# Heads of 16 and layer 0's experts: six call sites of a tiled matrix product, four pieces of 32 columns in place of two of 64

## The chip, the cores and the metric

The kernel runs on one core of one Trainium2 chip. Its time is the device time of one execution in microseconds (us). Five engines work side by side and meet at semaphores: TensorE (PE in the profile, its weight loads listed apart as PEld), VectorE (DVE), ScalarE (ACT), GpSimd (POOL) and SyncE (SP), which here mainly issues DMAs. Lower is better. All matrices are float32; the profile records each float32 matmul of the program as two weight loads and two matmuls.

## The reference, cut to what matters

A decoder of two layers on `x` of 8 batches x 256 tokens x 256 features. Each layer has self-attention with 16 heads of 16 features, a cross-attention to `ctx_2048`, and a mixture of experts. The part that the change touches:

```python
x = x + L0_attn(layernorm(x))     # q, k, v = x @ W.T + b; rope; softmax; @ Wo.T + bo
x = x + L0_xattn(ctx, layernorm(x))   # 16 heads of 16, no projections
x = x + L0_ffn(layernorm(x))      # below
x = x + L1_attn(layernorm(x))     # as L0_attn, causal, no biases
x = x + L1_xattn(layernorm(x), ctx)   # 16 heads of 64: not touched
x = x + L1_ffn(layernorm(x))      # 8 routed experts and a shared one: not touched

def L0_ffn(x):
    gates = einsum("bnd,de->bne", x, gate_w)
    t = log(clip(gates, 1e-6))
    for _ in range(8):            # Sinkhorn: columns, then rows
        t = t - logsumexp(t, axis=-2); t = t - logsumexp(t, axis=-1)
    vals, idx = top_k(swapaxes(exp(t), -1, -2), N // E)   # 32 tokens for each expert
    out = einsum("ebmd,edf->ebmf", x[idx], experts) * vals
    return zeros.at[idx].set(out)
```

## The kernel before

**Stages.** `plain` holds the whole work in order. Its first stage, up to about 467 us of the trace, runs 24 units: for each pair of batches of layer 0 two self-attentions and two cross-attentions, and then layer 1's eight self-attentions. Beside them go the experts of layer 0. After it come layer 1's cross-attention with heads of 64 and the last experts, which the change does not touch.

**One unit.** A unit (`SelfAttention` or `CrossAttention`, with a `Core`) has four steps, 0 to 3. In a step, `Core.scores` (L328, tile `st`) makes four matmuls of 32 rows x 128 columns of the array, 512 moving columns each; ScalarE takes the exponential of them (L339, tile `pT`); `Core.values` (L365, tile `o`) makes eight matmuls of 128 rows x 32 columns. One step's records are thus 8 of `st` and 16 of `o`. The scores of the next step are issued ahead of the values of this one, so that ScalarE's exponentials run beside TensorE's other work.

**What goes between.** All other TensorE work of the stage is put into these steps by hand: `beside(n, k, at, ...)` names a unit, a step and a place, `run(n, k, early)` issues what is planned (early: between scores and values; else after values). So the usual order on TensorE is scores, values, then whatever the plan put there, then the next scores. The order of all five engines in the stage is the order of the code (`tc.manual_schedule(engines=PINNED)`, L913). What is put there:

- `heads` (tile `qk`, 512 wide) and `vals` (tile `v`, 256 wide) through `projected`: x normalised and transposed, times Wq, Wk and Wv; `out` (tile `ao`, 256 wide): the attention's output times Wo, added to `x`.
- `transposed`, `begin`, `CrossAttention.out`: transposes on the full 128 x 128 array (tiles `tr`, `qps`, `qpsx`, `oR`).
- `chosen_experts`, a generator of which each `yield` ends a piece, one generator for two batches, so four in all: gates (tile `lg`, 8 wide), eight Sinkhorn iterations (tile `cs`, 16 wide, each a matmul with ones and then five operations on VectorE), the choice of tokens (VectorE and two DMAs), gathering the rows by a matmul with a one-hot matrix (tile `rps`), the experts themselves (tile `y`, L721, matmuls of 128 rows x 32 columns), and the return of the rows (tile `back`).

**The helper.** All products above but those of `st`, `o`, `y` and the transposes go through `product` (L274 to L278), whose matmuls all carry line L276. It cuts the 128 columns of the stationary operand `lhsT` in two halves of 64; each half is a matmul of its own, on its own half of the array's columns and of the output's partitions. `start` and `stop` open and close the accumulation. `product` is used in the later stages too (tiles `k`, `v<-wkv_x`, `h`, `wo`, `sc` and others), by call sites that stay as they are.

Of the kernel before, what the change touches and what calls it, by code (L numbers as in the profile page):

```python
# [39 lines left out]
P = 128  # L40
# [3 lines left out]
HP = 32  # L44
CTX = 512
XH, XD = 16, 64
E = 8
# [110 lines left out]
def plain(  # L158
# [4 lines left out]
    nc = tc.nc  # L163
# [53 lines left out]
    ones = const.tile([P, P], F32, name="ones")  # L217
# [46 lines left out]
    def layernorm_T(b, work, mm, bufs=2):  # L264

        xn = work.tile([P, 2, D], F32, tag="xn", name="xn", bufs=bufs)
        mv, rs = norm_stats([x[:, 2 * b + t, :] for t in range(2)], 1e-5, small, "ln")
        for t in range(2):
            last = normed(xn[:, t, :], x[:, 2 * b + t, :], mv, rs, t)
        return last, transposed(xn, work, mm, "xnT", bufs=bufs)  # L270
# [3 lines left out]
    def product(out, lhsT, rhs, start, stop):  # L274
        return [
            nc.tensor.matmul(out[h], lhsT[:, h], rhs, start=start, stop=stop, skip_group_check=True)  # L276
            for h in (slice(0, 64), slice(64, P))
        ]  # L278

    def transposed(rows, work, mm, tag, dst=None, bufs=2):  # L280

        ps = mm.tile([P, 2, 2 * P], F32, tag="mm", name="tr")
        for t in range(2):
            for c in range(2):
                nc.tensor.transpose(ps[:, c, t * P : (t + 1) * P], rows[:, t, c * P : (c + 1) * P], ident)  # L285
        if dst is None:
            dst = work.tile([P, 2, 2 * P], F32, tag=tag, name=tag, bufs=bufs)
        nc.scalar.copy(dst, ps)  # L288
        return dst
# [130 lines left out]
    class SelfAttention:  # L420
# [17 lines left out]
        def rows(self):  # L438
            self.xnT = transposed(self.xn, work, mm, "xnT")
            self.qkr = work.tile([P, 2, 2 * D], F32, tag="qkr", name="qkr")  # L440

        def projected(self, ps, t, lo, hi):
            for c in range(2):
                product(ps, self.xnT[:, c, bass.ts(t, P)], self.w[:, c, lo:hi], c == 0, c == 1)

        def heads(self, t):
            qk = mm.tile([P, 2 * D], F32, tag="mm", name="qk")
# [16 lines left out]
        def begin(self):  # L464
            kT = transposed(self.qkr[:, :, D:], work, mm, "kT")
            qps = mm.tile([P, 2, S], F32, tag="mm", name="qps")
            for t in range(2):
                for c in range(2):
                    nc.tensor.transpose(qps[:, c, bass.ts(t, P)], self.qkr[:, t, bass.ts(c, P)], ident)
            qm = masked_queries(work, qps, mask2)  # L470
            mine = dens[:, 2 * self.layer, 2 * self.b : 2 * self.b + 2]
            self.core = Core(kT, qm, self.v_pad, 1.0 / math.sqrt(HD), self.layer == 1, None, mine)
# [7 lines left out]
        def out(self, t):  # L480
            b, attT = self.b, self.core.attT
            xt = x[:, 2 * b + t, :]
            ps = mm.tile([P, 2 * D], F32, tag="mm", name="ao")[:, :D]
            for c in range(2):
                product(ps, attT[:, c, bass.ts(t, P)], self.wo[:, c, :], c == 0, c == 1)
            nc.vector.tensor_tensor(xt, xt, ps, ALU.add)


# [102 lines left out]
    gate = one.tile([P, 2, E], F32, name="gate")  # L591
# [35 lines left out]
    def chosen_experts(b0, nb):  # L627

        xn = bwork.tile([P, 2 * nb, D], F32, tag="xnb", name="xnb")
        g = bwork.tile([P, nb, 2, E], F32, tag="g", name="g")  # L630
# [10 lines left out]
        for b, xnT in enumerate(xnTs):  # L641
            lg = mm.tile([P, 2, D], F32, tag="mm", name="lg")
            for t in range(2):
                for c in range(2):
                    product(lg[:, t, :E], xnT[:, c, bass.ts(t, P)], gate[:, c, :], c == 0, c == 1)
            nc.vector.tensor_scalar(g[:, b], lg[:, :, :E], 1e-6, None, ALU.max)
            yield

        gt = bwork.tile([P, 2, nb, E], F32, tag="gt", name="gt")
        for it in range(8):  # L650
            cs = mm.tile([P, nb, E], F32, tag="mm", name="cs")
            for t in range(2):
                product(cs, ones, g[:, :, t, :], t == 0, t == 1)
            rc = bwork.tile([P, nb, E], F32, tag="rc", name="rc")
            nc.vector.reciprocal(rc, cs)
            nc.vector.tensor_tensor(g, g, rc.unsqueeze(2).to_broadcast([P, nb, 2, E]), ALU.mult)
            rsum = bwork.tile([P, nb, 2], F32, tag="rsum", name="rsum")
            nc.vector.tensor_reduce(rsum, g, AX.X, ALU.add)
            rr = bwork.tile([P, nb, 2], F32, tag="rr", name="rr")
            nc.vector.reciprocal(rr, rsum)  # L660
            dst = gt.rearrange("p t b e -> p b t e") if it == 7 else g
            nc.vector.tensor_tensor(dst, g, rr.unsqueeze(3).to_broadcast([P, nb, 2, E]), ALU.mult)
            yield
# [36 lines left out]
        def picked(b):  # L700
            pick = bwork.tile([P, 2, S], F32, tag="pick", name="pick")
            for t in range(2):
                nc.gpsimd.tensor_scalar(pick[:, t, :], idx_row[:, b, :], tokid[:, t : t + 1], None, ALU.is_equal)
            picks.append(pick)
# [3 lines left out]
        for b in range(nb):  # L708
            pick, put = picks[b], bwork.tile([P, 2, S], F32, tag="put", name="put")
            rps = mm.tile([P, 2, S], F32, tag="mm", name="rps")  # L710
            for c in range(2):
                for t in range(2):
                    product(rps[:, c, :], xn[:, 2 * b + t, bass.ts(c, P)], pick[:, t, :], t == 0, t == 1)
            rT = bwork.tile([P, 2, S], F32, tag="rT", name="rT")
            rows_made = nc.scalar.copy(rT, rps)
            yield
            y = mm.tile([P, 2, D], F32, tag="mm", name="y")
            for e in range(E):
                rows = slice(TOP * (e % 4), TOP * (e % 4) + TOP)
                for c in range(2):  # L720
                    nc.tensor.matmul(  # L721
                        y[rows, e // 4, :],
                        rT[:, c, TOP * e : TOP * (e + 1)],
                        experts[:, e, c, :],
                        start=c == 0,
                        stop=c == 1,
                    )
            for h in range(2):
                q = 2 * b + h
                junk = bwork.tile([P, S], F32, tag="junk", name="junk")  # L730
                for made in (
                    nc.gpsimd.tensor_scalar(put[:, h, :], num, col[:, 0, q : q + 1], None, ALU.is_equal),
                    nc.vector.scalar_tensor_tensor(
                        junk,
                        idx_row[:, b, :],
                        col[:, 0, q : q + 1],
                        later[:, h, :],
                        ALU.is_equal,
                        ALU.mult,
                        accum_out=over[:, q : q + 1],  # L740
                    ),
                ):
                    tc.add_manual_dep(made.ins, rows_made.ins.name, apart, reason="one entry's at a time")
            of_b = slice(2 * b, 2 * b + 2)
            nc.vector.tensor_scalar(weight[:, of_b], over[:, of_b], 0.0, None, ALU.is_equal)
            nc.vector.tensor_tensor(weight[:, of_b], weight[:, of_b], col[:, 1, of_b], ALU.mult)
            ys = bwork.tile([P, 2, D], F32, tag="ys", name="ys")
            for h in range(2):
                q = 2 * b + h
                nc.vector.tensor_scalar(ys[:, h, :], y[:, h, :], weight[:, q : q + 1], None, ALU.mult)  # L750
            if b + 1 < nb:
                picked(b + 1)
            yield
            back = mm.tile([P, 2, D], F32, tag="mm", name="back")
            for t in range(2):
                for h in range(2):
                    product(back[:, t, :], put[:, h, bass.ts(t, P)], ys[:, h, :], h == 0, h == 1)
            xb = x[:, 2 * (b0 + b) : 2 * (b0 + b) + 2, :]
            nc.vector.tensor_tensor(xb, xb, back, ALU.add)
            yield  # L760
# [93 lines left out]
    for n, u in enumerate(units):  # L854
# [28 lines left out]
    start = begun + (  # L883
        (0, 2, EARLY), (0, 3, 40), (0, 3, 41), (1, 0, 70), (1, 2, 70),
        (1, 3, 70), (2, 0, 15), (2, 1, 5), (2, 2, 10), (2, 2, 70), (2, 3, 70), (3, 0, 70), (3, 1, 45),
        (3, 2, 70), (3, 3, 85),
    )
# [1954 lines left out]
```

## Time and profile before

| | |
|---|---|
| median of 3 runs | 1226.51 us (1221.11 to 1227.33) |
| the profiled execution's own time | 1223.53 us |
| its span, first to last instruction | 1221.8 us |
| instructions | 28741 |
| PE busy in the span | 1152.2 us, 94% |
| PE busy from 10 to 470 us | 418.30 of 460 us, 4266 matmul records |
| of it the records of line L276 | 170.25 us, 1400 records |
| DVE / ACT / POOL busy from 10 to 470 us | 294.51 / 242.25 / 213.18 us |

In rows of instruction groups, a form such as `128*64 128x256` is a matmul on 128 rows and 64 columns of the array with 256 moving columns; matmuls on different columns of the array run side by side. "x256 | 33.4, 387" is 256 records, in whose union the engine was busy 33.4 us, 387 ns each. Since records overlap, the time that a record costs is the busy time over the count (or the distance of two starts), not its own duration. In the timeline, consecutive records of one kind are merged into one row with its start, its length and its count.

### The profile page before, as it was taken

The page shows a single profiled execution, that of the slowest core. Times are in us where ns is not written, and L with a number is a line of the kernel's source. Part 1 is how long each engine was busy: PE and PEld are TensorE (multiplying, and loading weights), DVE is VectorE, ACT ScalarE, POOL GpSimd, SP SyncE. Part 2 cuts the span into 40 slices and gives each one's busy share as a digit, 9 for nine tenths or more (in the row PEclk, how much of TensorE's full clock was granted, in tenths as well). Part 3 has the DMA queues.
Part 4 walks back from the last instruction along what each step waited for, and adds up shares of the span by engine and source line. Part 5 has one row for each costly group of instructions (what it writes and reads, how often), then busy time and mean ns, then how long its engine had stood idle before and what let it go on. Part 6 is the DMA issues. An engine that isn't in the chain of part 4 may idle for free.

```text
span 1221.8 us, 28741 instructions
## 1 busy us (share of the span) xinstructions
PE 1152.2 (94%) x12188; PEld 710.1 (58%) x12188; DVE 563.1 (46%) x1564; ACT 447.9 (37%) x696; POOL 416.9 (34%) x482
## 2 busy tenths in 40 slices
PE   5899989999898998999999999999999999999996
PEld 2334444444454444576666666666666576888874
DVE  4455767757776656223332423333335474222113
ACT  2666655656334351223232323232323231222220
POOL 2334344442736642032423333241416115000013
PEclk8999999999999999999999999999999999999999
DMA  7036232040200330010101010101012108599934
GB/s 221 1 119 211 89 104 93 10 169 1 82 1 11 104 132 2 18 37 18 36 19 37 18 36 19 36 19 36 19 37 72 35 6 322 233 393 410 378 104 128
DMA packets 51434, 116.58 MB, mean 95 GB/s; under 512 B 8272, under 2 KB 36416, under 8 KB 46944
## 3 DMA queue, kind: packets, MB, share of 16 engines
q1 hardware_dynamic: 45120, 98.90, 23.7%
q0 software_dynamic: 3456, 12.73, 2.9%
q10 hardware_dynamic: 2720, 3.02, 0.7%
q8 instruction: 98, 1.61, 0.5%
q14 instruction: 40, 0.33, 0.1%
HBM read 104.00 MB, written 27.93 MB: 108 GB/s over the span
## 4 chain that ended last, share of the span: by engine, by line
PE 75%; POOL 7%; DVE 7%; issue 5%; ACT 3%; DMA 1%; SPq 0%; POOLq 0%; DVEq 0%; ACTq 0%
PE v L276 7%; PE h L276 7%; PE k L276 6%; PE wo L276 5%; PE ox L1452 5%; PE stx L1413 4%; PE st L328 4%; PE out L1830 4%; PE qk L276 3%; PE o L365 3%; PE h L1035 3%; PE out L1647 3%; PE q L276 3%; PE tr L285 2%; PE fm L276 2%
## 5 line engine op out<-in xcount | busy, mean ns | idle before, releaser
L339 ACT ACTIVATE pT<-st 128x1024 f32<-128x1024 f32 (+1 forms) x128 | 110.5, 917 | 83.0 <-PE st L328 82.2
L365 PE MATMUL o<-pT,padv 128*32 128x256 f32 (+1 forms) x1536 | 100.0, 372 | 3.2 <-POOL pT L344 3.1
L1419 POOL TENSOR_TENSOR both<-pTx 128x512 f32<-128x512 f32 x64 | 82.1, 1309 | 48.9 <-issue 43.2
L365 PEld LDWEIGHTS o<-pT,padv 128*32 128x32 f32 x1536 | 40.8, 110 | 86.3 <-issue 41.7
L276 PE MATMUL h<-xrT,w 128*64 128x128 f32 (+1 forms) x1936 | 87.2, 250 | 2.9 <-issue 2.9
L258 POOL TENSOR_TENSOR lnrs<-lnve,mhalf 128x2 f32<-128x2 f32 x48 | 34.7, 724 | 157.2 <-DVE lnve L256 152.8
L276 PEld LDWEIGHTS h<-xrT,w 128*64 128x64 f32 x1936 | 84.5, 137 | 5.9 <-issue 3.7
L339 ACT ACTIVATE pT<-st,kbias 128x1024 f32<-128x1024 f32 x64 | 67.8, 1112 | 40.2 <-PE st L328 40.2
L1417 ACT ACTIVATE pTx<-stx 128x1024 f32<-128x1024 f32 x64 | 62.1, 1021 | 41.3 <-PE stx L1413 26.2
L1028 DVE TENSOR_TENSOR midr<-sl,h 128x128 f32<-128x128 f32 x102 | 29.4, 288 | 102.2 <-PE h L276 68.6
L328 PE MATMUL st<-qm,kT 32*128 32x512 f32 (+1 forms) x512 | 69.1, 610 | 5.1 <-ACT pT L339 3.2
L1027 ACT ACTIVATE sl<-h 128x128 f32<-128x128 f32 (+1 forms) x114 | 35.3, 310 | 99.3 <-PE h L276 58.5
L276 PE MATMUL qk<-l_wqkv,xnT 128*64 128x512 f32 x256 | 65.4, 634 | 2.2 <-ACT xnT L288 2.2
L1413 PE MATMUL stx<-qTx,kTx 64*128 64x256 f32 x512 | 64.3, 391 | 2.5 <-ACT pTx L1417 2.5
L1452 PE MATMUL ox<-pTx,vx 128*64 128x256 f32 x512 | 62.3, 385 | 0.0
L1507 POOL TENSOR_TENSOR oT<-oT,rs 128x512 f32<-128x512 f32 x30 | 37.7, 1290 | 67.0 <-DMA rs<-rd 67.0
L258 POOL TENSOR_TENSOR lxrs<-lxve,mhalf 128x2 f32<-128x2 f32 x8 | 5.6, 703 | 153.5 <-DVE sc L1166 123.3
L276 PE MATMUL wo<-wout_x,oT 128*64 128x256 f32 x512 | 58.0, 379 | 0.0
L1413 PEld LDWEIGHTS stx<-qTx,kTx 64*128 64x128 f32 x512 | 46.1, 186 | 20.3 <-ACT pTx L1417 7.2
L344 POOL TENSOR_SCALAR_AFFINE_SELECT pT<-pT 128x512 f32<-128x512 f32 x64 | 41.5, 661 | 41.8 <-ACT pT L339 41.8
L1452 PEld LDWEIGHTS ox<-pTx,vx 128*64 128x64 f32 x512 | 33.9, 136 | 26.4 <-issue 12.1
L1460 DVE COPY oT<-ox 128x512 f32<-128x512 f32 x16 | 11.1, 691 | 81.0 <-PE ox L1452 81.0
(361 smaller groups left out, 2198.3 us busy)
## 6 DMA issues: line engine op xcount, KB each, us to landing
w<-packs SPq DMA_DIRECT2D x22, 1408.0 KB
w<-packs SPq DMA_DIRECT2D x22, 768.0 KB
rs<-rd SPq DMA_DIRECT2D x16, 512.0 KB
packs<-L_ffn_w_eDF SPq DMA_DIRECT2D x8, 704.0 KB
packs<-L_ffn_w_eDF SPq DMA_DIRECT2D x8, 640.0 KB
packs<-L_ffn_w_eFD SPq DMA_DIRECT2D x8, 640.0 KB
ctxT<-ctx_T SPq DMA_DIRECT2D x8, 512.0 KB
wkv_x<-L_xattn_Wkv POOLq DMA_DIRECT2D x1, 4096.0 KB
```

What stands on the lines that cost most here:

```text
L258: nc.gpsimd.tensor_tensor(rs[:, :n], ve[:, :n], mhalf[:, :n], ALU.pow)
L276: nc.tensor.matmul(out[h], lhsT[:, h], rhs, start=start, stop=stop, skip_group_check=True)
L328: nc.tensor.matmul(st[:, r, :, :n], self.kT[rows, c, bass.ts(kt, P)], self.qm[rows, :, c, q0:], start=True, stop=True,)
L339: nc.scalar.activation(pT[:, :, :, :n], st[:, 2 * k : 2 * k + 2, :, :n], AF.Exp, scale=self.scale, **kb)
L344: nc.gpsimd.affine_select(out=pT[:, :, :, :P], in_=pT[:, :, :, :P], compare_op=ALU.is_ge, fill=0.0, base=0, pattern=[[0, 2], [0, 2], [1, P ...
L365: nc.tensor.matmul(o[HP * j : HP * j + HP, m, q0:], self.v_pad[:, kt, 8 * c + 2 * j + m, :], pTs[j // 2][:, j % 2, m, : S - q0], start=kt ...
L1413: nc.tensor.matmul(st[:, g, kt, :], kT[rows, c, bass.ts(kt, P)], qT[rows, c, :], start=True, stop=True)
L1417: nc.scalar.activation(pT, st, AF.Exp, scale=scale)
L1419: nc.gpsimd.tensor_tensor(both, pT[:, :, 0, :], pT[:, :, 1, :], ALU.add)
L1452: nc.tensor.matmul(o[XD * g : XD * (g + 1), i, :], v[:, kt, 2 * (c2 + i) + g, :], pT[:, g, kt, :], start=kt == 0, stop=kt == 1, skip_group ...
L1507: engines[c2 % 4 // 2].tensor_tensor(oT[:, c2 : c2 + 2, :], oT[:, c2 : c2 + 2, :], rs[:, c2 : c2 + 2, :], ALU.mult)
L1830: nc.tensor.matmul(ps[h], mid[:, i, h], sets[k % len(sets)][1][:, i, :], start=i == 0, stop=i == NFC - 1, skip_group_check=True,)
```

## The change

A second helper, `product4`, cuts the stationary operand in four pieces of `HP` = 32 columns, each with its own quarter of the array's columns and of the output's partitions. It issues four matmuls where `product` issues two, with the same moving operand, and the arithmetic is the same. Six call sites use it in place of `product`; by tile they are `qk` and `v` (both layers' self-attention), `ao`, `lg`, `cs`, `rps` and `back`. Nothing is moved and no other engine's instruction changes.

```diff
+    def product4(out, lhsT, rhs, start, stop):
+        for h in range(0, P, HP):
+            nc.tensor.matmul(
+                out[h : h + HP], lhsT[:, h : h + HP], rhs, start=start, stop=stop, skip_group_check=True
+            )
+
...
         def projected(self, ps, t, lo, hi):
             for c in range(2):
-                product(ps, self.xnT[:, c, bass.ts(t, P)], self.w[:, c, lo:hi], c == 0, c == 1)
+                product4(ps, self.xnT[:, c, bass.ts(t, P)], self.w[:, c, lo:hi], c == 0, c == 1)
...
             for c in range(2):
-                product(ps, attT[:, c, bass.ts(t, P)], self.wo[:, c, :], c == 0, c == 1)
+                product4(ps, attT[:, c, bass.ts(t, P)], self.wo[:, c, :], c == 0, c == 1)
...
                 for c in range(2):
-                    product(lg[:, t, :E], xnT[:, c, bass.ts(t, P)], gate[:, c, :], c == 0, c == 1)
+                    product4(lg[:, t, :E], xnT[:, c, bass.ts(t, P)], gate[:, c, :], c == 0, c == 1)
...
             for t in range(2):
-                product(cs, ones, g[:, :, t, :], t == 0, t == 1)
+                product4(cs, ones, g[:, :, t, :], t == 0, t == 1)
...
                 for t in range(2):
-                    product(rps[:, c, :], xn[:, 2 * b + t, bass.ts(c, P)], pick[:, t, :], t == 0, t == 1)
+                    product4(rps[:, c, :], xn[:, 2 * b + t, bass.ts(c, P)], pick[:, t, :], t == 0, t == 1)
...
                 for h in range(2):
-                    product(back[:, t, :], put[:, h, bass.ts(t, P)], ys[:, h, :], h == 0, h == 1)
+                    product4(back[:, t, :], put[:, h, bass.ts(t, P)], ys[:, h, :], h == 0, h == 1)
```

## The prediction

> **What bounds the kernel now.** I read the page first, then the engines' busy time in the stage that holds every changed product, TensorE's timeline there, its groups by form, and last what TensorE waits for.
>
> ```profile
> PE 1152.2 (94%) x12188; PEld 710.1 (58%) x12188; DVE 563.1 (46%) x1564; ACT 447.9 (37%) x696; POOL 416.9 (34%) x482
> ```
>
> TensorE is busy 94% of the span. The changed products run from 10 to 467 us. Busy time from 10 to 470 us (PE, PEld, DVE, ACT, POOL, with counts):
>
> ```profile
> 10.00:470.00 460.00, 418.30 (x4266) 196.28 (x4264) 294.51 (x875) 242.25 (x323) 213.18 (x250) 0.98 0.26 85
> ```
>
> No other engine passes 64% here. But "busy" holds bubbles, and the timeline shows them (start, length, kind; from one start to the next is what a group costs):
>
> ```profile
> 195.55 1.07 PE L365 MATMUL o<-pT,padv 128*32 128x256 f32 x16
> 196.55 0.41 PE L276 MATMUL cs<-g,ones 128*64 128x16 f32 x8
> 196.80 1.93 PE L276 MATMUL ao<-l_wo,attT 128*64 128x256 f32 x16
> 198.66 1.14 PE L328 MATMUL st<-qm,memk 32*128 32x512 f32 x8
> ```
> ```profile
> 211.12 1.07 PE L365 MATMUL o<-pT,padv 128*32 128x256 f32 x16
> 212.12 1.94 PE L276 MATMUL qk<-l_wqkv,xnT 128*64 128x512 f32 x8
> 213.89 0.36 PE L276 MATMUL cs<-g,ones 128*64 128x16 f32 x8
> ```
> ```profile
> 260.78 1.07 PE L365 MATMUL o<-pT,padv 128*32 128x256 f32 x16
> 261.66 1.96 PE L721 MATMUL y<-experts,rT 128*32 128x256 f32 x32
> 263.56 0.64 PE L276 MATMUL lg<-gate,xnbT 128*64 128x8 f32 x16
> ```
> ```profile
> 607.60 3.60 PE L276 MATMUL v<-tw,sw 128*64 128x512 f32 x16
> 611.03 1.04 PE L276 MATMUL q<-xnT,wq_x 128*64 128x128 f32 x16
> ```
>
> The same `o` x16 costs 1.00 us before `qk` and before `cs`, which use the array in pieces of 64 columns, but 0.88 us before `y`, which uses pieces of 32 as `o` does. So a change of the array's division costs about 0.11 us in the group it follows. That is the quantity of this prediction.
>
> Groups by form over the whole span; busy time over count is the cost of a record:
>
> ```profile
> L276 PE MATMUL h<-xrT,w 128*64 128x64 f32 x880 | 27.1, 222 | 2.9 <-issue 2.9
> L721 PE MATMUL y<-experts,rT 128*32 128x256 f32 x256 | 15.8, 383 | 0.5 <-DVE qs L412 0.5
> L276 PE MATMUL back<-ys,put 128*64 128x256 f32 x128 | 15.5, 384 | 2.9 <-DVE ys L750 2.4 <-ACT padv L301 0.6
> ```
>
> Weight loads, from 0 to 470 us:
>
> ```profile
> L365 PEld LDWEIGHTS o<-pT,padv 128*32 128x32 f32 x1536 | 40.8, 110 | 86.3 <-issue 41.7 <-POOL pT L344 9.8 <-DVE att L385 5.3
> L276 PEld LDWEIGHTS cs<-g,ones 128*64 128x64 f32 x256 | 11.6, 137 | 13.7 <-issue 9.2 <-DVE g L662 1.5 <-ACT xnT L288 1.0
> ```
>
> TensorE's longest waits in the stage (total, times, longest):
>
> ```profile
> PE st L328 <- ACT pT L339: 7.8, 8, 1.5
> PE tr L285 <- DVE qkr L457: 6.5, 7, 1.6
> PE cps L692 <- DMA by_half<-slots: 5.8, 3, 2.2
> PE qpsx L541 <- DVE xnx L262: 3.9, 4, 1.1
> ```
>
> **What the Trainium skill says.** TensorEngine Tiling (Array Packing), section Tiling Modes: changing the tiling mode, not just the tile, drains TensorE. The trace agrees: 1.00 against 0.88 us above. The same page's Performance Considerations give each matmul an overhead of about 60 cycles, so that very few columns cost as much as 60; here a pair of records costs 58 ns at 16 columns and 62 ns (2 x 30.8) at 64. TensorE: Matmul & The Clock Gate, section on LDWEIGHTS: the load time follows the number of columns, columns/1.2 ns, so 27 ns for 32 and 53 for 64. The trace agrees: 137 - 110 = 27 ns for 32 columns more. The same page's Part 3 lets column tiles run side by side with some 4 ns for each tile more. Trace: a set of four records of `y` costs 4 x 15.8/256 = 0.247 us and a pair of `back` 2 x 15.5/128 = 0.242 us, bubbles included: no loss for four at 256 columns.
>
> **The change part by part.** I call the records that run side by side a set: two records before, four after. A set of 512 columns takes 0.429 us (`v<-tw,sw`: 3.43 us for 8 sets), one of 256 takes half, 0.215.
>
> 1. The products themselves at 512 and 256 columns (`qk`, `v`, `ao`, `rps`, `back`). The number of sets stays; each has four records. At 256 columns `y` shows no extra cost. At 512 no division by 32 is in the trace; it can't stream faster than 0.429, and double weight loads and issues have twice the room, so I take 0. Bounds: 0 and +0.015 us for each of the 128 sets of `qk` (8 ns for each of two records more, twice the page's price), +1.9 us.
>
> 2. Changes of division on the way in. I went through the timeline from 10 to 467 us and counted uninterrupted runs of changed products. There are 86: 68 follow a group of 32 columns (`o`, sometimes `y`), 18 follow transposes or the like. For the 68 the change of division goes: 0.11 us each, 7.5 us. With it goes a second loss: after a change, the first set cannot have the second's weights loaded behind a running matmul. `qk` x8 costs 1.77 us, where 4 x 0.429 is 1.72: 0.05 us. Of the 68, 53 begin with wide products, 2.7 us; 15 begin with `cs` or `lg`, where the four sets of `cs` cost 0.25 us against 4 x 0.058, 0.02 each: 0.3 us. Sum -10.5 us.
>
> 3. On the way out. In 8 runs the next group is of the array's full height (7 of them `y` or `o`, division 32): -0.12 us for the 7, -0.9. The other 78 still change, and now from 32 columns: `o` to `qk` costs 0.11 where `ao` to `st` costs 0.10 (16 records: 1.86 - 8 x 0.215 - 0.03): +0.01 each, +1.0 us. For the 18 that come from transposes the first set's loss shrinks by the 27 ns of 32 columns fewer: -0.5 us.
>
> 4. `cs` and `lg`. They have 128 + 64 = 192 sets, at 58 ns each. At 16 and 8 columns the stream is short, and the load of 64 columns (54 ns by the difference above) sets the pace. With 32 columns it is 27 ns, and the loads of different column groups run side by side, as those of `o` must to keep its sets at 0.215. I take 32 ns: -26 ns for each of 192 sets, less some that stand first in a run, -4.5 us. Bounds: if the matmul's overhead or the issue of eight instructions sets the pace, 58 ns or more; at 15 ns for each instruction (30.8 ns for a load and a matmul of `h`, the densest stream in the trace) 116 ns, which is +11 us. I lean to the low end[...].
>
> Other engines: no instruction is added, moved or removed, no DMA, no queue. The semaphore waits stay: the first of four waits for what the first of two waited for, the last one releases what the last of two did. Results come 0.01 us later inside a set.
>
> TensorE's own work thus shrinks by 10.5 + 0.9 - 1.0 + 0.5 + 4.5 = 15.4 us over 96 steps, 0.16 us a step.
>
> **What is given back.** TensorE still waits in the stage: 44 waits of 41 us together from 10 to 470 us, none over 2.2 us. Where a wait ends a chain that TensorE itself began (products, then VectorE's rotation and GpSimd's sum, then `tr`), saving between the chain's beginning and its end only makes the wait longer. Such chains span one to three steps, and `st <- ACT pT` one step. I take one step's saving, 0.16 us, for each of the 44 waits: 7.0 us. Bounds: 2 (the waits are few in time, most saving is made elsewhere) and 12 (three steps for most waits, and new waits where slack is under 0.2 us). Net -8.4 us. After 470 us TensorE hardly waits, so the saving reaches the end.
>
> Against the profiled execution's 1223.5 us that is 1215.1. The median of the runs shown is 3 us above it, with runs from 1221.1 to 1227.3; -8.4 from the median gives 1218.1. I predict 1216.5, between the two.
>
> **Rivals.** (a) The other engines' chains eat nearly all: in the chain of waits, GpSimd's normalisations and VectorE's ranking stand beside TensorE around 190 to 240 us. Then -15.4 + 12 = -3: about 1221 us. For it: 44 waits in 96 steps. Against: most saving is made in steps where TensorE doesn't wait. (b) Hardly anything is eaten: -15.4 + 2 = -13, 1211 us. For it: waits hold only 41 of 460 us. (c) Slower: TensorE's sequencer becomes the bound in `cs` and `lg`, whose sets hold eight instructions. The gain without part 4 is 10.9 us, so slower by 0.5% (6.1 us) needs +17 us on 192 sets, 89 ns each: 147 ns a set, 18 ns an instruction. At 25 ns it would be 200 ns a set, +27 us, net +16: 1240 us. Against: `h` keeps 15 ns over 880 records. (d) The change of division is not what costs 0.11, and `o` before `qk` waits for something else; then only part 4 remains, about 1221 as in (a). Against: the same 0.11 stands before `cs`, with other operands.
>
> **How the numbers follow.** A measurement of this kernel can tell about 0.5% (6 us) from no change. Forecast (1213 to 1220): 0.50. (a) and (d) together: 0.24; (b): 0.17; (c): 0.09. Faster by over 0.5% means under 1220.4 against the median: nearly all of the forecast, all of (b), a little of (a): 0.68. Within 0.5%: most of (a) and the edge of the forecast, 0.24. Slower: (c), 0.08. The range leaves out (c) and the tail of (b) and takes in (a) with the scatter of 3 us: 1208 to 1225. The likeliest case's own range is 1213 to 1220.
>
> **What would show it.** Right: in the changed timeline `o` x16 costs 0.88 us before `qk`, `v`, `ao` or `cs`; `qk` x16 costs 1.72 us; `cs` x16 costs 0.13 to 0.2 us; `st` after a product costs the same; TensorE's total wait from 10 to 470 us rises from 41 to about 48 us and line L276's busy time falls. Wrong: `qk` sets over 0.44 us (part 1), `o` still at 1.00 (part 2), `cs` at over 0.4 us (part 4), or waits risen by over 12 us.

## The result, and the profile after

Six runs of the changed kernel have a median of 1216.02 us (1214.46 to 1217.34), six of the kernel before 1222.74 us (1217.11 to 1227.33). The ratio is 0.9938 with a 95% interval of 0.9916 to 0.9960: 7.6 us faster, 4.9 to 10.3 (the medians differ by 6.7). The profiled executions took 1214.46 and 1223.53 us.

TensorE's timeline in the changed kernel, at the places that the prediction read before (start, length, kind):

```profile
186.96 1.07 PE L371 MATMUL o<-pT,padv 128*32 128x256 f32 x16
187.84 1.91 PE L282 MATMUL back<-ys,put 128*32 128x256 f32 x32
189.57 1.91 PE L282 MATMUL rps<-pick,xnb 128*32 128x256 f32 x32
191.30 0.29 PE L282 MATMUL cs<-g,ones 128*32 128x16 f32 x16
191.52 1.14 PE L334 MATMUL st<-qm,memk 32*128 32x512 f32 x8
...
197.51 0.29 PE L282 MATMUL cs<-g,ones 128*32 128x16 f32 x16
197.63 2.00 PE L727 MATMUL y<-experts,rT 128*32 128x256 f32 x32
...
207.90 1.07 PE L371 MATMUL o<-pT,padv 128*32 128x256 f32 x16
208.79 1.90 PE L282 MATMUL qk<-l_wqkv,xnT 128*32 128x512 f32 x16
210.51 0.29 PE L282 MATMUL cs<-g,ones 128*32 128x16 f32 x16
```

From start to start, `o` now costs 0.88 us before `back` and 0.89 before `qk` (1.00 before). `qk` costs 1.72 (1.77 before), and is twice as many records. `cs` costs 0.12 us before `y`, which is 31 ns for a set, and 0.22 before `st`, where a change of division remains. Where nothing was changed, nothing moved: `o` before the transpose `tr` costs 1.00 us in both kernels (34.99 to 35.99 us before, 33.10 to 34.10 after). So the pieces of the prediction can be seen one by one.

Busy time from 10 us to the idle time before the stage's last `ao`, which begins at 463.25 us in place of 471.07, 7.8 us sooner (PE, PEld, DVE, ACT, POOL):

```profile
10.00:461.00 451.00, 405.42 (x5666) 191.97 (x5658) 292.48 (x873) 241.93 (x323) 214.25 (x250) 0.98 0.26 87
```

TensorE has 1400 records more and is busy 12.9 us less. Its largest waits in the same stretch:

```profile
PE st L334 <- ACT pT L345: 8.5, 8, 1.5
PE tr L291 <- DVE qkr L463: 7.8, 7, 1.7
PE cps L698 <- DMA by_half<-slots: 6.8, 3, 2.9
PE qpsx L547 <- DVE xnx L262: 4.3, 4, 1.1
PE o L371 <- POOL pT L350: 4.2, 5, 1.6
```

Each of the four shown before has grown (7.8, 6.5, 5.8, 3.9). All waits of the stretch sum to 45.6 us against 40.7 (10 to 470 us of the kernel before): 4.9 us of the saving was turned into waiting.

The end of the stage shows a loss that the prediction had no term for. Tile `nvw` is a product that the change doesn't touch; its group before, and then after:

```profile
L833 PE MATMUL nvw<-wout_x,nvs 128*128 128x256 f32 x16 | 3.7, 384 | 0.7 <-PE ao L276 0.7
```
```profile
L839 PE MATMUL nvw<-wout_x,nvs 128*128 128x256 f32 x16 | 5.4, 511 | 0.7 <-PE ao L282 0.7
```

The same work took 1.7 us more. The busy time of this stretch of the changed kernel tells why; the number before the DMA's share is the granted clock:

```profile
465.00:468.40 3.40, 3.40 (x9) 2.69 (x10) 0.46 (x6) 0.00 (x0) 0.47 (x1) 0.53 0.02 2
```

TensorE ran at half its clock for about 3.4 us. `nvw` began at 472.81 us before and at 464.99 after, 7.8 us sooner; 1.7 of that went back in `nvw`. The other 3 us of the profiled executions' 9.1 lie at the end: 1.0 in the last experts, 1.9 after the last matmul. The change does nothing there, so these 3 us belong to the two executions and not to the change.

### The profile page after: what moved, and what is told of

Its sections match the earlier page's. It is cut to its first block, busy times and chain, and to the rows that moved or that the text cites. A ratio compares the mean times of both kernels' runs of the same rounds, so it can differ in the third digit from the quotient of the medians.

```text
span 1212.7 us, 31559 instructions
## 1 busy us (share of the span) xinstructions
PE 1141.0 (94%) x13596; PEld 707.9 (58%) x13596; DVE 562.4 (46%) x1564; ACT 447.6 (37%) x696; POOL 417.2 (34%) x482
## 3 DMA queue, kind: packets, MB, share of 16 engines
q8 instruction: 109, 1.79, 0.6%
## 4 chain that ended last, share of the span: by engine, by line
PE 73%; POOL 8%; DVE 7%; issue 6%; ACT 3%; DMA 2%; SPq 0%; POOLq 0%; ACTq 0%; DVEq 0%
PE h L276 7%; PE k L276 6%; PE v L276 6%; PE wo L276 5%; PE ox L1458 5%; PE stx L1419 4%; PE out L1836 4%; PE out L1653 3%; PE st L334 3%; PE h L1041 3%; PE o L371 3%; PE qk L282 3%; PE q L276 3%; PE tr L291 2%; PE fm L276 2%
## 5 line engine op out<-in xcount | busy, mean ns | idle before, releaser
L282 PE MATMUL qk<-l_wqkv,xnT 128*32 128x512 f32 x512 | 63.9, 616 | 2.2 <-ACT xnT L294 2.2
```

What stands on the lines that cost most here:

```text
L282: nc.tensor.matmul(out[h : h + HP], lhsT[:, h : h + HP], rhs, start=start, stop=stop, skip_group_check=True)
```

## The experiments

Two theories. **Match**: what counts is whether a product divides the array as its neighbours do; the short sets of `cs` and `lg` add to it. **Pace**: the short sets run faster, and the divisions cost nothing. All runs were timed beside the kernel before.

**Only the wide products in four pieces** (`cs` and `lg` in two):

```diff
-                    product4(lg[:, t, :E], xnT[:, c, bass.ts(t, P)], gate[:, c, :], c == 0, c == 1)
+                    product(lg[:, t, :E], xnT[:, c, bass.ts(t, P)], gate[:, c, :], c == 0, c == 1)
...
-                product4(cs, ones, g[:, :, t, :], t == 0, t == 1)
+                product(cs, ones, g[:, :, t, :], t == 0, t == 1)
```

> Only the wide products (qk, v, ao, rps, back) in four pieces; cs and lg stay in two. Theory of the match (what counts is whether the group before and after divides the array in the same way): 30 changes of division fewer than before, by the costs read in the trace of before 5.3 us of TensorE less; about half is given back in waits, so 2 to 4 us faster than before (some 1220). Rival, the theory of the pace (the short sets of cs and lg run faster, divisions cost nothing): wide sets keep their pace, so no change against before.

**Only `cs` and `lg` in four pieces**: the other four call sites back to `product`.

> Only cs and lg in four pieces, the wide products in two. Match: the short sets save 5 us, but 11 changes of division more than before are made, since cs and lg now differ from the products beside them: 3.4 us of TensorE less, 1 to 3 us faster than before. Pace: the whole gain of the change, 6 to 7 us, is here. If the match is right, this and the wide products alone add up to 8.7 us of TensorE's work, and both together to 16.1, because each group's neighbours then match too.

Ratios to before: wide 0.9998 (0.9986 to 1.0010), narrow 0.9994 (0.9981 to 1.0007). Alone, neither moves the time by anything that can be told from zero (-0.2 and -0.7 us); together they are worth 7.6 us. Pace falls: the short sets alone don't bring the gain. Of the sizes expected of match, that of the wide products (2 to 4) was missed, and that of the narrow (1 to 3) lies in part within its interval (2.3 faster to 0.9 slower).

TensorE's own work shows what the times don't. Its busy time up to the start of `nvw`, in the kernel before, wide alone, narrow alone and the changed kernel:

```profile
0.00:472.80 472.80, 420.76 (x4278) 197.73 (x4279) 302.32 (x899) 244.32 (x326) 215.93 (x260) 0.98 0.26 87
0.00:470.81 470.81, 415.62 (x5302) 194.51 (x5303) 302.23 (x899) 244.12 (x326) 217.11 (x260) 0.98 0.27 88
0.00:471.76 471.76, 418.23 (x4662) 193.63 (x4663) 302.56 (x899) 244.48 (x326) 216.30 (x260) 0.98 0.26 87
0.00:464.98 464.98, 408.03 (x5686) 193.29 (x5687) 301.55 (x899) 244.00 (x326) 217.00 (x260) 0.99 0.27 89
```

Wide alone saves 5.1 us of it (5.3 by count), narrow alone 2.5 (3.4 by count), and both together 12.7, which is more than the sum. That is what match says. `nvw` begins 2.0 and 1.0 us sooner than before, but there it meets half clock in both kernels, and takes 6.6 and 6.5 us in place of 3.7 (wide, then narrow):

```profile
L839 PE MATMUL nvw<-wout_x,nvs 128*128 128x256 f32 x16 | 6.6, 601 | 0.6 <-PE ao L282 0.6
L839 PE MATMUL nvw<-wout_x,nvs 128*128 128x256 f32 x16 | 6.5, 590 | 0.6 <-PE ao L276 0.6
```

In these two executions the clock thus took back what had been won. The timed runs point the same way. Runs of one kernel differ with their mean granted clock: of 50 runs of the kernel before, one at 0.994 took 1216.66 us and one at 0.986 took 1228.61. The mean clock was 0.9908 for the kernel before, 0.9890 for wide and 0.9895 for narrow. An estimate by one straight line through the runs of this series (1.0 us for each 0.001 of clock) puts both some 2 us below the kernel before at the same clock. Whether the lower clock belongs to these two kernels or to chance stays open.

The timelines show why the two need each other. Wide alone:

```profile
194.09 1.07 PE L371 MATMUL o<-pT,padv 128*32 128x256 f32 x16
195.09 0.41 PE L276 MATMUL cs<-g,ones 128*64 128x16 f32 x8
195.43 1.93 PE L282 MATMUL ao<-l_wo,attT 128*32 128x256 f32 x32
197.30 1.14 PE L334 MATMUL st<-qm,memk 32*128 32x512 f32 x8
```

Narrow alone:

```profile
195.08 1.07 PE L371 MATMUL o<-pT,padv 128*32 128x256 f32 x16
195.97 0.29 PE L282 MATMUL cs<-g,ones 128*32 128x16 f32 x16
196.19 1.95 PE L276 MATMUL ao<-l_wo,attT 128*64 128x256 f32 x16
198.07 1.14 PE L334 MATMUL st<-qm,memk 32*128 32x512 f32 x8
```

From `o` to `st` the kernel before takes 3.11 us, wide alone 3.21, narrow alone 2.99. Wide alone is slower there: `o` keeps its 1.00 us, and now `cs` costs 0.34 in place of 0.25, because it differs from `ao` too. The changed kernel takes 2.96 for the same row of work (from 192.59 to 195.55 us).

**A change of division put back inside each projection**, half of its contraction in two pieces:

```diff
-                product4(ps, self.xnT[:, c, bass.ts(t, P)], self.w[:, c, lo:hi], c == 0, c == 1)
+                (product, product4)[c == 0](ps, self.xnT[:, c, bass.ts(t, P)], self.w[:, c, lo:hi], c == 0, c == 1)
```

> As the changed kernel, but in qk and v the first half of the contraction in four pieces, the second in two: a change of division inside each of 64 products. Match: some 0.15 us for each, 10 us of TensorE more than the changed kernel, of which 4 to 8 reach the end: 1220 to 1224. In the timeline each of these products is 0.16 us longer. Pace: as the changed kernel, 1216.

Ratio 0.9985 (0.9969 to 1.0001), so 5.7 us slower than the changed kernel, within the 4 to 8 expected (the median, 1219.51 us, is just under the range named; the interval reaches to the kernel before). In its trace TensorE is busy for 419.96 us up to `nvw`, 11.9 more than in the changed kernel, where 10 were expected. Its timeline:

```profile
208.56 1.07 PE L371 MATMUL o<-pT,padv 128*32 128x256 f32 x16
209.45 1.04 PE L282 MATMUL qk<-l_wqkv,xnT 128*32 128x512 f32 x8
210.42 1.08 PE L276 MATMUL qk<-l_wqkv,xnT 128*64 128x512 f32 x4
211.43 0.32 PE L282 MATMUL cs<-g,ones 128*32 128x16 f32 x16
```

`o` stays at 0.89, and `qk` costs 1.98 us against 1.72. That is 0.26, not the 0.16 expected, since going back to 32 columns for `cs` is a second change. Where `st` follows, which divides the array in another way in any case, the same `qk` costs 0.15 us more (1.98, from 72.77 to 74.75 us, against 1.83, from 72.71 to 74.54 in the changed kernel). Only the division differs, and with it the number of instructions, so this prices it directly.

**The six call sites as one matmul of 128 columns** (`product4` makes a single call).

> The six call sites as one matmul of all 128 columns. Match: o to product is a change of division again; products next to transposes match them; the loads of 128 columns take 109 ns for each short set. 7.5 us of TensorE more than before, 3 to 8 us slower than before. Rival (fewer instructions are better, the division doesn't count): no slower than before.

Ratio 1.0060 (1.0035 to 1.0085), 7.4 us slower than before, within the 3 to 8 expected. Fewer instructions do not help. In its trace `o` costs 1.00 us before `qk` (213.92 to 214.92 us), as in the kernel before, and four sets of `cs` cost 0.44 us (216.74 to 217.18). A part of the loss can be the clock: up to `nvw` this trace stands at half clock for 27.0 us, that of the kernel before for 17.1.

**The same idea where the profile shows it next**: in layer 1's cross-attention `den` has 32 columns and `ox`, right after it, 64.

```diff
-                        for g in range(2):
+                        for g, w in ((0, 0), (0, HP), (1, 0), (1, HP)):
                             nc.tensor.matmul(
-                                o[XD * g : XD * (g + 1), i, :],
-                                v[:, kt, 2 * (c2 + i) + g, :],
+                                o[XD * g + w : XD * g + w + HP, i, :],
+                                v[:, kt, 2 * (c2 + i) + g, w : w + HP],
                                 pT[:, g, kt, :],
```

> The changed kernel, and in layer 1's cross-attention ox in halves of 32 columns too, next to den, which has 32: 33 changes of division fewer, 5.0 us of TensorE less. TensorE hardly waits in this stage, so nearly all arrives: 4 to 5 us faster than the changed kernel (1211 to 1212). If four pieces help only in the first stage: 1216.

1209.51 us, ratio 0.9901 (0.9885 to 0.9917): 4.5 us below the changed kernel by the ratios, as expected (the median is below the range named). From the profile of this kernel:

```profile
581.11 0.64 PE L1434 MATMUL den<-both,hot 128*32 128x256 f32 x8
581.57 1.91 PE L1458 MATMUL ox<-pTx,vx 128*32 128x256 f32 x32
583.29 0.61 PE L1434 MATMUL den<-both,hot 128*32 128x256 f32 x8
583.73 1.91 PE L1458 MATMUL ox<-pTx,vx 128*32 128x256 f32 x32
```

`den` costs 0.46 and `ox` 1.72 us here; in the changed kernel the same two cost 0.57 (579.12 to 579.69) and 1.88 (579.69 to 581.57). In a stage where TensorE hardly waits, nearly the whole saving (5.0 us by count) arrives: from the end of `nvw` to the last matmul, all at full clock, this trace takes 731.7 us and that of the changed kernel 735.8.

**What was given back.** The next kernel is the last one, with the piece of the experts that opens with `cps` issued later:

```diff
-        (4, 1, 85), (4, 2, EARLY), (4, 3, 70), (5, 1, 10), ...
+        (4, 1, 85), (4, 2, EARLY), (5, 0, EARLY), (5, 1, 10), ...
-        (4, 1, 84), (4, 1, 85), (4, 3, 20), (5, 0, 50), ...
+        (4, 1, 84), (4, 1, 85), (4, 3, 60), (5, 0, 50), ...
```

> The kernel with ox in halves of 32, and the piece of the first experts that begins with the transposes cps is issued later: for three of four pairs of batches one step or half a step on, so that TensorE doesn't stand waiting for the DMA by_half (3 waits, 6.2 us together). If the saving was given back in waits of this kind: the three waits shrink by 3 to 5 us, and 2 to 4 us reach the end (1206 to 1208). Rival, what was given back lies in chains that the later place only moves on (the picks on GpSimd, then rps, ys and back): the waits go to rps, y or back, and the time stays at 1210 or rises.

1209.04 us, but the kernel before was at 1225.66 in these runs: ratio 0.9862 (0.9845 to 0.9878), 4.8 us below the last one by the ratios, 3.6 us by the two spans (that of the last kernel is the slowest of its five runs), but only 0.5 us by the medians. The waits for `by_half`:

```profile
PE cps L698 <- DMA by_half<-slots: 4.2, 3, 1.8
```

They fell from 6.2 to 4.2 us, less than the 3 to 5 expected, and no other wait grew (`back` 3.0 and `rps` 0.5 in both). `nvw` begins at 463.56 us in place of 467.21. So in the traces this part of what was given back sat in the place of one piece, not in a chain that only moves. How much of it reaches the time stays open: the two kernels ran in different series, in which the kernel before itself took 1222.01 and 1225.66 us, and the median missed the range named. Its median is the lowest of all versions tried.

**Four pieces for every product of the helper.**

> The changed kernel, and the other products of the helper (features, keys and values of layer 1's cross-attention, its output, router and routed experts) in four pieces too. Match: these have hardly a neighbour of 32 columns, 0.5 us of TensorE less than the changed kernel, so 1216. Rival, four pieces are better wherever they stand: several us faster. Rival, the sequencer can't feed eight instructions in the 58 ns of a set of h (64 columns): each of its 440 sets gets longer; at 10 ns for an instruction 80 ns, 10 us slower.

1270.24 us, ratio 1.0349 (1.0302 to 1.0397), 50 us slower than the changed kernel by the ratios (1226.88 x 0.0411). The rival of the sequencer's limit was nearest, but its mechanism was wrong too: the groups of `h` kept their pace and stood still in between. At full clock a set of four records with 64 moving columns takes 56 ns from start to start (median), where a set of two took 58; at half clock it takes 107. The rows below mix the two clocks, so 36.1 us for 440 sets give 82 ns.

```profile
L276 PE MATMUL h<-xrT,w 128*32 128x128 f32 x2112 | 61.5, 273 | 5.8 <-issue 5.8
L276 PE MATMUL h<-xrT,w 128*32 128x64 f32 x1760 | 36.1, 253 | 22.9 <-issue 22.7
```

**Only `h` in four pieces**:

```diff
-                        product(h[:, bass.ts(i, n)], w13[:, c, lo : lo + P], xrT[:, c, bass.ts(i, n)], c == 0, c == 1)
+                        product4(h[:, bass.ts(i, n)], w13[:, c, lo : lo + P], xrT[:, c, bass.ts(i, n)], c == 0, c == 1)
```

> The changed kernel, and of the other products only h, the routed experts' first, in four pieces. With all products in four pieces, h stood still 22.7 us and more at its 64-column sets, by a wait that the profile puts down to nothing (issue), though its sets ran at the same pace between the pauses. If the pauses come from the supply of TensorE's instructions while the weights w stream in (each packet of instructions 16 KB, 256 of them): 25 to 35 us slower than the changed kernel (1241 to 1251), and no pause in the cross-attention. Rival, a limit of the sequencer at each instruction: the sets themselves get longer.

1264.1 us, ratio 1.0312 (1.0295 to 1.0329), 46 us slower than the changed kernel: more than the 25 to 35 expected. Its timeline in the routed experts:

```profile
1057.83 1.97 PE L282 MATMUL h<-xrT,w 128*32 128x64 f32 x122
1063.62 3.52 PE L282 MATMUL h<-xrT,w 128*32 128x64 f32 x128 [3.82 <-issue]
1067.37 1.65 PE L282 MATMUL h<-xrT,w 128*32 128x64 f32 x102 [0.22 <-issue]
```

Between two pauses stand 128 records, each with its weight load: 256 instructions. And the DMA queue of instructions carried 11 packets more in the changed kernel (109 against 98) for 2818 instructions more (31559 against 28741): 256 to a packet. In the routed experts this trace has 17 pauses of over 0.2 us; the count of TensorE's instructions from one to the next is a multiple of 256 each time, to within one, and a packet of that queue landed 1.2 to 1.6 us before each pause ended. So TensorE stands still until the next packet of its own program has come. There is no such pause in the cross-attention, as expected, and the rival falls: the sets take 56 ns at full clock here too. The pauses of `h` sum to 32.3 us; the clock adds to them, 0.94 granted between 1044 and 1259 us against 1.00 in the changed kernel's same stage.

## Why the prediction was right

The time (1216.5 forecast, 1216.02 measured) and the mechanism held, but two terms were too large and cancelled, so that the nearness of the two numbers is in part luck. By its steps:

- **Part 1**, no loss in the wide products: right, also for the 512 columns that no trace had shown. `qk` costs 4 x 0.43 us.
- **Part 2**, 0.11 us for the change of division and 0.05 for the weights of the second set: right, 0.88 to 0.89 us for `o` and 1.72 for `qk`. That the second loss is one of loading weights fits its growth with the columns: about 0.02 us with 32 (`qk` before `st` in the changed kernel: 1.85 us after a transpose, from 229.80 to 231.65, against 1.83 after `o`), 0.05 with 64, 0.10 with 128 (1.82, from 214.92 to 216.74 in the kernel with one matmul). The kernels with divisions put back and with divisions taken from `ox` moved the time as this price says.
- **Part 3**, the way out: right where it can be read. `cs` before `y` loses its change; before `st` 0.22 - 4 x 0.031 = 0.10 remains.
- **Part 4**, 32 ns for a short set: 31 measured. The bound of 58 or more, and with it rival (c) for this change, is excluded; the limit that (c) feared exists elsewhere, as the supply of instructions.
- **What is given back**, 7.0 us by one step's saving for each wait: too large, the waits grew by 4.9. It was a rough size between bounds of 2 and 12. TensorE's own work was too large as well: its busy time up to `nvw` fell by 12.7 us, not by 15.4. The two errors cancel: 15.4 - 7.0 = 8.4 was forecast, and 12.7 - 4.9 = 7.8 is what `nvw` came sooner. The clock does not explain the missing 2.7. Up to `nvw` the kernel before stands at half clock for 17.1 us and the changed one for 13.7, mainly because its first stretch, at about 20 us, lasts 10.2 us before and 3.4 after; so up to 1.7 of the 12.7 can be the clock's and not the change's. Which part was counted too high was not settled.
- **The base**: the forecast stood on runs of the kernel before at 1223.5 and 1226.5 us, and beside the changed kernel it took 1222.74. That the saving was smaller too (7.6 for 8.4) brought the number home.
- Rivals (a) and (b), nearly all or hardly anything given back: neither. Rival (d), that `o` before `qk` waits for something else than the division, fell with the divisions put back.

Not foreseen: that the parts alone would not show in the times. The count of changes was near for each alone (5.1 us of TensorE's work for 5.3, 2.5 for 3.4), but how much of a saving reaches the end also hangs on where the stretches at half clock fall, and the prediction had no term for them.

## What to carry to other kernels

Look at what stands before and after a matmul on TensorE, not at the matmul: where neighbours divide the array differently, each change cost 0.11 us and 0.05 more for the weights behind it, and dividing a product as its neighbours do was free at 256 and 512 columns. Convert a whole run of neighbours; where one of two was changed alone a border stayed, and the two parts saved 5.1 and 2.5 us of TensorE's work in place of 12.7 together. Don't cut finer where short matmuls follow each other densely: in `h`, with 64 moving columns and four pieces, the program itself came too slowly. When two kernels differ by a few us, look at the granted clock of the runs before calling the difference nothing or something.

## What the runs showed of the hardware that was not expected

- TensorE's instructions arrive in packets of 16 KB (1.79 MB in 109 packets), 256 instructions each, and a dense stream can use them up sooner than they come: pauses of up to 3.8 us in the kernel with `h` in four pieces, some 32 us in all. Two such pauses, of 1.6 and 1.4 us, already stand in the kernel before.
- Changes of the array's division within one accumulation, half of the contraction in four pieces and half in two, cost no more than between two products: 0.26 us for two changes.
- TensorE's granted clock is either full or half in all ten traces. Apart from the one at the end of each trace, a stretch at half clock lasts 3.41 us or a multiple of it. Within one execution the stretches begin on one grid of 3.41 us, and where this grid lies differs between executions. The stretches follow times with many waits: there are 55, and in the 3.41 us before each TensorE was busy for at most 57%, in 52 of them for at most 50%. Before the stretch that met `nvw` in the changed kernel it was 1.28 of 3.41 us:

```profile
461.79:465.20 3.41, 1.28 (x17) 0.66 (x18) 3.41 (x15) 0.00 (x0) 0.55 (x1) 1.00 0.00 0
```

In the kernel before, nearly the same waits lay differently on the grid, 1.59 us busy from 467.46 to 470.87, and no half clock followed. So waits that stand close together can cost up to 1.7 us (half of 3.41, an estimate) beyond themselves, and whether they do changes from run to run. This is read from the traces; no experiment moved the waits to try it.
